# Graph layers on one core: the row of f by way of DRAM, the next batch taken up sooner, other buffer counts

## The chip, the core and the metric

The kernel runs on one core of a Trainium2 chip. Time is device microseconds (us) from start to end of one launch. The median of three runs of the kernel before is 2380.97 us (2374.90 to 2388.02). One further execution was taken with the hardware profiler; every row below comes from that one.

The core has five engines that run side by side, each through its own list of instructions in order: TensorE (PE, matrix products and transposes), VectorE (DVE), ScalarE (ACT), GpSimd (POOL) and SyncE (SP). SP only issues DMA transfers; POOL here issues the indexed ones (gathers and scatters), ACT the stores of the output. An instruction whose inputs are not there yet stops everything behind it on its own engine.

## The reference

Two graph layers on x of 16 batches x 1024 nodes x 256 features, with one 1024 x 1024 matrix `adj` that has few entries other than zero.

```
# layer 0, for each batch
feats  = data @ W1.T
f1     = feats @ W2 + b2[0]
logits = f1[:, None] + f1[None, :]
coefs  = softmax(leaky_relu(logits) + bias1, axis=-1)      # bias1 = adj
h      = coefs @ feats + bias2 + data
# layer 1, for each batch
hidden = relu((h @ W1[:d])[:, None, :] + (h @ W1[d:])[None, :, :] + b1)
S      = sigmoid(hidden @ W2 + b2)
a_t    = (S * adj).T @ h
m_t    = (adj.T @ h) * h
z      = beta1*h + beta2*(a_t @ Wa + ba) + beta3*(m_t @ Wm + bm)
```

Layer 0 is dense: each batch has a softmax over 1024 x 1024 logits. Each logit is a sum of one number per row and one number per column, so a tile of 128 rows of logits needs f of its own rows as a column (one number per partition, `f99`) and f of all 1024 nodes as a row that stands in every partition (`frow`). In layer 1, S is only needed where `adj` is not zero, so it is computed edge by edge.

## The kernel before

**Order.** The kernel writes its own schedule. A planner (`Timetable`) keeps a clock, `times.now`, that counts only PE's matmuls. Helpers such as `transposes`, `attention`, `one_end` put a PE step at `times.now` and move the clock on; what must follow on other engines is put at a due time after it (`times.at`). At the end all entries are emitted in order of due time. So the due times set the order of instructions on each engine, and nothing else; the hardware waits for whatever is late.

**Dense stage.** Batches 0 to 15 run one after the other. A batch `b` has these steps on PE:

- `begin(b, h)`: two times eight transposes of x into `xT` (L891). The tile of x, `xh` (`held[b]`), is loaded by `load_x` (L439) and later overwritten by h; there are two such tiles.
- `begin_features(b, c2)`, four times: products of `xT` with `w1T` (L926), whose last column gives f. `keep_features` cuts f to `f99` on DVE (L939), takes an exponential and scales on ACT (L943, L951).
- `begin_f(b)`: eight transposes of `f99`, broadcast, put f as a row into all 128 partitions in PSUM (`pr`, L911); ACT copies that to `frow` with a constant added (L919).
- for each of eight tiles of rows: `before` (ACT L962 adds f of the row and takes a relu, DVE L969 adds `adj`, ACT L975 takes the exponential), `transposes` (L981, copied to `eT` by ACT L985), `attention` (L991), and `keep_h` on DVE (L1002, L1005) which makes h.
- for each of four pairs of tiles: `turned_ends` (L1011, copied to `hT` by ACT L1022), `one_end` twice (L1028, stored to `pu_d` and `pw_d` through the doubled tiles `end0` and `end1`), `weigh_ends` (L1058, stored to `ha_d` through the doubled tile `ea`).
- `messages` (L1090) and `products` (L1110, DVE L1120 writes `zb`, which SP stores to `zb_d`). They read `held[b]` to the end.

The steps are interlaced: the last tiles of batch `b` run while batch `b+1` is turned and gets its features, and the messages and products of batch `b-1` run inside batch `b`. Batches 0 to 3 and 14 (`LATER`) are put off: h goes to DRAM (`put_off`, L1079), and their messages and products come much later, after `take_up` (L1083) has loaded h again. PSUM has two pools: `p1` with four tiles and `p2` with two; `begin`, `begin_features`, `begin_f` and `transposes` all use `p2`.

**Scores.** As soon as a group of four batches has its `pu_d` and `pw_d`, POOL gathers rows of them for 540 tiles of edges (L1144, L1151, eight buffers `gv`), DVE compares (L1180), DVE or ACT sums up (L1191, L1194), and POOL scatters the results to `sa_d` (L1160). This runs beside the dense stage from 386 us on, on all engines but PE.

**Gathering.** After the dense stage, for each group in the order 1, 2, 0, 3 and each of eight columns of tiles (`vc`), PE multiplies with S*adj in four parts (`gather`, L1284). Each part needs a piece of `sa_d` (`load_sa`, L1254, five buffers), turned so that the batches stand apart (`part_sa`, ACT L1267), weighed with `adj` on DVE (`weigh_sa`, L1272), and two tiles of `ha_g` (`load_ha`, L1249, `HA` = 11 buffers of 4 KB per partition, eight tiles to a group). The put-off messages and products stand between these parts (`follows`). Every column ends with `finish_z` (L1305) and a store.

At the end of a batch, PE's order before the change is: transposes 4, turned_ends 0, attention 3, transposes 5, attention 4, turned_ends 1, begin(b+1, 0), both_ends 0, begin(b+1, 1), transposes 6, attention 5, both_ends 1, features 0, transposes 7, attention 6, turned_ends 2, features 1, features 2, one_end(2, 0), features 3, half_end(2, 1, 0), attention 7, begin_f(b+1).

Of the kernel before, what the change touches and what calls it, by code (L numbers as in the profile page):

```python
# [14 lines left out]
P = 128  # L15
# [355 lines left out]
def edge_layers(  # L371
# [65 lines left out]
    def load_x(b):  # L437
        held[b] = dense.tile([P, C, D], F32, name="xh", bufs=2)
        nc.sync.dma_start(out=held[b], in_=x_view[b])  # L439
# [197 lines left out]
    ha_d = [dram.tile([N, G * D], F32, name=f"ha_d{g}") for g in range(NG)]  # L637
    h_d = {b: dram.tile([P, C * D], F32, name=f"h_d{b}") for b in LATER}
    zb_d = [dram.tile([N, G * D], F32, name=f"zb_d{g}") for g in range(NG)]

# [276 lines left out]
    def keep_f(b):  # L917
        st["frow"] = work.tile([P, N], F32, name="frow")
        nc.scalar.activation(st["frow"], st.pop("pr"), AF.Identity, bias=b2_s)  # L919

    def features(b, c2):
        pf = st["pf", c2] = p2.tile([P, 2, BANK], F32, tag="p2", name="pf")
        for i in range(2):
            c = 2 * c2 + i
            for h in range(H):
                nc.tensor.matmul(  # L926
                    pf[:, i, : D + 1],
                    lhsT=st["xT"][:, h, c * P : (c + 1) * P],
                    rhs=w1T[:, h, :],
                    start=(h == 0),  # L930
                    stop=(h == H - 1),
                )
# [148 lines left out]
    def take_up(b):  # L1081
        held[b] = dense.tile([P, C, D], F32, name="xh", bufs=2)
        nc.sync.dma_start(out=held[b].rearrange("p c d -> p (c d)"), in_=h_d[b])  # L1083
# [51 lines left out]
    AHEAD = 6  # L1135
    HA = 11
    SA = 5
# [123 lines left out]
    def part_sa(g, vc, part):  # L1261
# [4 lines left out]
        )  # L1266
        nc.scalar.copy(apart, sat.rearrange("p c v g -> p c g v"))  # L1267

# [57 lines left out]
    def begin_f(b):  # L1326

        end = times.matmuls(1024, lambda: rows_of_f(b))
        times.at(end + 0.1, lambda: keep_f(b))
        for c in range(3):  # L1330
            before(b, c, end + 1.5 + 2.5 * c)

    def begin_features(b, c2):
        end = times.matmuls(4 * (D + 1), lambda: features(b, c2))
        times.at(end + 0.3, lambda: keep_features(b, c2))

    def before(b, c, time):
# [59 lines left out]
    for b in range(B):  # L1397
# [28 lines left out]
        if b == 0:  # L1426
            for i in range(2):
                end_of = times.matmuls(512, lambda i=i: turn_columns(i))
                times.at(end_of + 0.3, lambda i=i: keep_columns(i))

        transposes(b, 2)
        before(b, 5, times.now)
# [15 lines left out]
        attention(b, 2)  # L1448
        time = products(b - 1, 2, 3) if at_once else times.now
        if more:  # L1450
            times.at(time, lambda b=b: load_x(b + 1))
        else:
            times.at(time, lambda: take_up(LATER[0]))

        transposes(b, 4)
        before(b, 7, times.now)
        turned_ends(b, 0)
        attention(b, 3)

        transposes(b, 5)  # L1460
        attention(b, 4)
        turned_ends(b, 1)
        if more:
            begin(b + 1, 0)
        both_ends(b, 0)

        if more:
            begin(b + 1, 1)
        transposes(b, 6)
        attention(b, 5)  # L1470
        both_ends(b, 1)
        if more:
            begin_features(b + 1, 0)

        transposes(b, 7)
        attention(b, 6)
        turned_ends(b, 2)
        if more:
            begin_features(b + 1, 1)
            begin_features(b + 1, 2)  # L1480
        else:
            times.now += 1.0
        one_end(b, 2, 0)
        if more:
            begin_features(b + 1, 3)
        half_end(b, 2, 1, 0)

# [115 lines left out]
    for n, (g, c) in enumerate((g, c) for g in order for c in range(C)):  # L1603
        if n < C:
            due = lead + 2.0 + PACE * (n + n // 2 + 1)
        elif n < HA:
            due = when[2 + n - C] + 0.1
        else:
            k, c1 = divmod(n - HA, C)
            due = when[C * 2 * k + (15 if c1 < C // 2 else 16)] + 0.1  # L1610
        times.at(due, lambda g=g, c=c: load_ha(g, c))
# [73 lines left out]
```

## Time and profile before

| what | value |
|---|---|
| three runs, median | 2380.97 us |
| profiled execution, whole | 2388.68 us |
| its span, first to last instruction | 2387.0 us |
| mean granted TensorE clock | 0.961 |
| moved by DMA | 638.19 MB, 267 GB/s over the span |
| `frow` written (L919), first of batch 1, batch 4, batch 5, batch 15 | 98.86, 306.92, 383.99, 1604.38 us |
| from one `frow` to the next, batches 1 to 4 | 69.1 to 69.6 us |
| from one `frow` to the next, batches 6 to 15 | 110 to 130 us, mean 122 us |
| gathering, first L1284 to the end | 1775.98 to 2387 us |

The busy time of PE is modelled from the start of each matmul, so a PE that is shown as busy need not be at its peak. The granted clock is the share of full speed at which the throttle let PE run in a stretch. In the rows, "a <- b" names what ended an engine's idle time.

### The profile page before, as it was taken

Reading aid. Unit: us, or ns where it says so; the run is one execution under the profiler, and the core shown is the slowest. Engines: PE = TensorE matmul, PEld = TensorE weight load, DVE = VectorE, ACT = ScalarE, POOL = GpSimd, SP = SyncE. Lnnn points to the kernel's source line nnn. Section 1 sums busy time; section 2 is a strip of 40 time slices with the busy share of each in tenths; the row PEclk is TensorE's granted clock in tenths of the full one; section 3 lists DMA queues with packets and bytes.
Section 4 is the critical chain, followed back from the end, with each engine's and each line's share of the span. In section 5 each row is a group of like instructions: output and inputs, shape, how many; then the busy total and the mean of one; then the engine's idle time right before and its main releaser. Section 6 shows DMA issues by size and latency. Waiting matters only on the chain.

```text
span 2387.0 us, 30406 instructions
## 1 busy us (share of the span) xinstructions
PE 2193.2 (92%) x9478; PEld 1684.9 (71%) x9478; DVE 1729.9 (72%) x2660; ACT 1467.0 (61%) x3820; POOL 1376.8 (58%) x1277
## 2 busy tenths in 40 slices
PE   7999999898987899999897998988889999999998
PEld 6888877676665576666675766667557768778687
DVE  6699658777776777777685777767558888879544
ACT  5544567475746565656474656657347778779554
POOL 2223125677775767666776666767656776777400
PEclk9999999999999999999998999989999999999999
DMA  6789887777776777777776777778799999999664
GB/s 235 272 313 335 307 319 234 233 231 237 241 235 208 234 223 241 227 229 233 225 247 228 236 217 221 230 220 272 255 322 392 354 354 404 340 395 405 228 213 150
DMA packets 282491, 638.19 MB, mean 267 GB/s; under 512 B 43218, under 2 KB 142546, under 8 KB 281042
## 3 DMA queue, kind: packets, MB, share of 16 engines
q0 software_dynamic: 109312, 349.81, 46.1%
q1 hardware_dynamic: 154450, 268.93, 31.2%
q10 hardware_dynamic: 18560, 17.44, 2.2%
q8 instruction: 77, 1.26, 0.2%
q14 instruction: 92, 0.75, 0.1%
HBM read 476.42 MB, written 159.78 MB: 267 GB/s over the span
## 4 chain that ended last, share of the span: by engine, by line
PE 59%; DVE 17%; another core or an unknown queue 6%; issue 6%; ACT 5%; DMA 4%; POOL 1%; SPq 0%; POOLq 0%; DVEq 0%; ACTq 0%
PE pzg L1284 16%; PE pm L1090 12%; PE pv L991 10%; PE pp L1028 7%; DVE gv L1180 6%; PE pf L926 3%; PE pz L1110 3%; PE pea L1058 3%; DVE lg L1191 2%; PE pt L981 2%; DMA xh<-in_x_dram 2%; DVE e L969 2%; ACT gv L1194 2%; ACT e L962 1%
## 5 line engine op out<-in xcount | busy, mean ns | idle before, releaser
L1151 POOL DMA_INDIRECT gv<-pw_d,idx_v x540 | 591.7, 1096 | 398.9 <-ACT gv L1194 200.0
L1194 ACT ACTIVATE gv<-gv 128x272 f32<-128x272 f32 x1380 | 576.5, 421 | 348.3 <-DVE gv L1180 216.1
L1180 DVE TENSOR_TENSOR gv<-gv,gu 128x544 f32<-128x544 f32 x1080 | 735.0, 719 | 0.0
L1160 POOL DMA_INDIRECT sa_d<-lg,idx_s x540 | 620.2, 1148 | 185.7 <-issue 154.3
L991 PE MATMUL pv<-feats,eT 128*128 128x257 f32 x2048 | 479.4, 385 | 26.7 <-issue 14.5
L1284 PE MATMUL pzg<-ha_g,apart 128*128 128x256 f32 x2048 | 452.0, 382 | 16.8 <-issue 9.6
L1090 PE MATMUL pm<-adj_sb,xh 128*128 128x512 f32 x1024 | 455.8, 599 | 7.9 <-issue 7.9
L991 PEld LDWEIGHTS pv<-feats,eT 128*128 128x128 f32 x2048 | 385.0, 192 | 93.6 <-issue 27.3
L1284 PEld LDWEIGHTS pzg<-ha_g,apart 128*128 128x128 f32 x2048 | 390.4, 191 | 81.6 <-issue 18.5
L1090 PEld LDWEIGHTS pm<-adj_sb,xh 128*128 128x128 f32 x1024 | 195.0, 192 | 236.9 <-issue 234.8
L1028 PE MATMUL pp<-wuv,hT 128*128 128x272 f32 x1024 | 274.6, 416 | 40.0 <-ACT hT L1022 18.3
L1267 ACT COPY apart<-sat 128x1024 f32<-128x1024 f32 x128 | 263.5, 2063 | 65.7 <-PE pzg L1284 51.4
L1028 PEld LDWEIGHTS pp<-wuv,hT 128*128 128x128 f32 x1024 | 200.7, 202 | 93.4 <-ACT hT L1022 23.8
L1194 ACT ACTIVATION_READ_ACCUMULATOR gv<-gv 128x1 f32 x1380 | 262.3, 190 | 0.0
L1191 DVE TENSOR_REDUCE lg<-gv 128x4 f32<-128x1088 f32 x195 | 250.5, 1284 | 5.3
L1272 DVE TENSOR_TENSOR apart<-apart,adj_sb 128x1024 f32<-128x1024 f32 x128 | 156.7, 1224 | 107.9 <-ACT apart L1267 91.9
L969 DVE CUSTOM_DVE_ANT_0 e<-e,adj_sb 128x1024 f32<-128x1024 f32 x128 | 156.2, 1222 | 89.3 <-ACT e L962 54.8
L962 ACT ACTIVATE e<-frow,f 128x1024 f32<-128x1024 f32 x128 | 146.6, 1146 | 94.1 <-remote 53.0
L829 POOL DMA_INDIRECT table_d<-rec,at x52 | 56.3, 1083 | 198.4 <-DVE rec L824 177.1
L985 ACT COPY eT<-pt 128x1024 f32<-128x1024 f32 x128 | 127.8, 999 | 52.6 <-remote 13.3
L975 ACT ACTIVATE e<-e,top 128x1024 f32<-128x1024 f32 x128 | 145.8, 1145 | 19.9 <-DVE top L969 19.3
L981 PE MATMUL pt<-ident,e 128*128 128x128 f32 x1024 | 137.2, 277 | 15.2 <-ACT e L975 8.1
(171 smaller groups left out, 1923.8 us busy)
## 6 DMA issues: line engine op xcount, KB each, us to landing
sa_d<-zero SPq DMA_DIRECT2D x128, 512.0 KB
sat<-sa_d SPq DMA_DIRECT2D x128, 512.0 KB
pu_d<-end SPq DMA_DIRECT2D x64, 272.0 KB
pw_d<-end SPq DMA_DIRECT2D x64, 272.0 KB
xh<-in_x_dram SPq DMA_DIRECT2D x16, 1024.0 KB
ha_d<-ea SPq DMA_DIRECT2D x64, 256.0 KB
zb_d<-zb SPq DMA_DIRECT2D x64, 256.0 KB
ha_g<-ha_d SPq DMA_DIRECT2D x32, 512.0 KB
```

Of the source, the lines that this page charges most:

```text
L969: nc.vector.tensor_tensor_reduce(e, e, adj_sb[:, c, :], -1.0, BIG, ALU.add, ALU.min, accum_out=top)
L981: nc.tensor.transpose(pt[:, j * P : (j + 1) * P], e[:, j * P : (j + 1) * P], ident)
L991: nc.tensor.matmul(pv[:, : D + 1], lhsT=eT[:, j, :], rhs=st["feats", b][:, j, :], start=(j == 0), stop=(j == C - 1),)
L1028: nc.tensor.matmul(pp[:, :R], lhsT=st["hTi", b, i][:, h, k * P : (k + 1) * P], rhs=wuv[:, side, h, :], start=(h == 0), stop=(h == H - 1),)
L1090: nc.tensor.matmul(pm, lhsT=held[b][:, c, h * P : (h + 1) * P], rhs=adj_sb[:, c, span], start=(c == 0), stop=(c == C - 1),)
L1151: nc.gpsimd.indirect_dma_start(out=gv, out_offset=None, in_=pw_d[g], in_offset=bass.IndirectOffsetOnAxis(ap=idx_v[:, t, s : s + 1], axis=0),)
L1160: dma = nc.gpsimd.indirect_dma_start(out=sa_d[g], out_offset=bass.IndirectOffsetOnAxis(ap=idx_s[:, t, s : s + 1], axis=0), in_=lg[:, i, :] ...
L1180: nc.vector.tensor_tensor(mv, mv, mu, op)
L1191: nc.vector.tensor_reduce(lg[:, i, :], one, AX.X, ALU.add)
L1194: nc.scalar.activation(one[:, j, :], one[:, j, :], AF.Copy, accum_out=lg[:, i, j : j + 1])
L1267: nc.scalar.copy(apart, sat.rearrange("p c v g -> p c g v"))
L1284: nc.tensor.matmul(st["pzg", g, vc][:, j, :], lhsT=apart[:, c, j, :], rhs=st["ha", g, 2 * part + c][:, j * D : (j + 1) * D], start=(part = ...
```

## The change

It has six parts.

1. For all batches but the first, `begin_f` no longer transposes f on PE and no longer copies it on ACT. Instead `spread_f`, right after the last features, adds the constant on DVE into a small tile `f_out`, and SP stores that to a row `f_d[b]` in DRAM; `take_f` loads that row into all 128 partitions of `frow`, also on SP. The `before` steps of the first three tiles are now due from the end of attention 7.
2. `xh` has three buffers instead of two, and `load_x(b+1)` is emitted ahead of transposes 2 instead of behind the last products of batch `b-1`.
3. The two `begin` steps move up: begin(b+1, 0) behind attention 3, begin(b+1, 1) behind turned_ends 1. The four `begin_features` are spread: behind transposes 6, behind attention 5, between the two ends of pair 1, and behind transposes 7.
4. The tail of the batch's order changes with that: pair 1's ends and weighing come between attention 5 and transposes 7, and turned_ends 2 comes before attention 6.
5. `ha_g` has nine buffers instead of eleven (two tiles of 4 KB make room for the third `xh` of 8 KB), and from the tenth load on its due time is 3.5 us after the start of the part that reads the buffer last.
6. `part_sa` reads `sat` in the order in which it lies and writes `apart` in steps of 128 elements; before, it read in steps of four elements and wrote in order.

```diff
-        held[b] = dense.tile([P, C, D], F32, name="xh", bufs=2)
+        held[b] = dense.tile([P, C, D], F32, name="xh", bufs=3)
...
+    f_d = [dram.tile([N, 1], F32, name=f"f_d{b}") for b in range(B)]
...
+    def spread_f(b):
+
+        f = two.tile([P, C], F32, name="f_out")
+        nc.vector.tensor_scalar(f, st["f99"], b2_s, None, ALU.add)
+        nc.sync.dma_start(out=f_d[b].rearrange("(c p) o -> p (c o)", p=P), in_=f)
+
+    def take_f(b):
+
+        st["frow"] = work.tile([P, N], F32, name="frow")
+        nc.sync.dma_start(
+            out=st["frow"], in_=f_d[b].rearrange("n o -> (n o)").partition_broadcast(P)
+        )
...
-    HA = 11
+    HA = 9
...
-        nc.scalar.copy(apart, sat.rearrange("p c v g -> p c g v"))
+        nc.scalar.copy(apart.rearrange("p c g v -> p c v g"), sat)
...
     def begin_f(b):
 
-        end = times.matmuls(1024, lambda: rows_of_f(b))
-        times.at(end + 0.1, lambda: keep_f(b))
+        if b == 0:
+            end = times.matmuls(1024, lambda: rows_of_f(b))
+            times.at(end + 0.1, lambda: keep_f(b))
         for c in range(3):
-            before(b, c, end + 1.5 + 2.5 * c)
+            before(b, c, times.now + 1.5 + 2.5 * c)
...
         times.at(end + 0.3, lambda: keep_features(b, c2))
+        if b and c2 == C // 2 - 1:
+            times.at(end + 0.6, lambda: spread_f(b))
+            times.at(end + 3.0, lambda: take_f(b))
...
+        if more:
+            times.at(times.now, lambda b=b: load_x(b + 1))
         transposes(b, 2)
...
-        time = products(b - 1, 2, 3) if at_once else times.now
-        if more:
-            times.at(time, lambda b=b: load_x(b + 1))
-        else:
-            times.at(time, lambda: take_up(LATER[0]))
+        if at_once:
+            products(b - 1, 2, 3)
+        if not more:
+            times.at(times.now, lambda: take_up(LATER[0]))
...
         attention(b, 3)
+        if more:
+            begin(b + 1, 0)
 
         transposes(b, 5)
         attention(b, 4)
         turned_ends(b, 1)
         if more:
-            begin(b + 1, 0)
+            begin(b + 1, 1)
         both_ends(b, 0)
 
-        if more:
-            begin(b + 1, 1)
         transposes(b, 6)
-        attention(b, 5)
-        both_ends(b, 1)
         if more:
             begin_features(b + 1, 0)
-
-        transposes(b, 7)
-        attention(b, 6)
-        turned_ends(b, 2)
+        attention(b, 5)
         if more:
             begin_features(b + 1, 1)
+        one_end(b, 1, 0)
+        if more:
             begin_features(b + 1, 2)
-        else:
-            times.now += 1.0
-        one_end(b, 2, 0)
+        one_end(b, 1, 1)
+        weigh_ends(b, 1)
+
+        transposes(b, 7)
         if more:
             begin_features(b + 1, 3)
+        turned_ends(b, 2)
+        attention(b, 6)
+        one_end(b, 2, 0)
         half_end(b, 2, 1, 0)
...
-            due = when[C * 2 * k + (15 if c1 < C // 2 else 16)] + 0.1
+            due = begins[order[k], C - 1, c1 // 2] + 3.5
```

More of the change, by code (lines that the diff above doesn't have):

```diff
@@ L1081, in take_up @@
     def take_up(b):
-        held[b] = dense.tile([P, C, D], F32, name="xh", bufs=2)
+        held[b] = dense.tile([P, C, D], F32, name="xh", bufs=3)
         nc.sync.dma_start(out=held[b].rearrange("p c d -> p (c d)"), in_=h_d[b])
```

## The prediction

> **What bounds the kernel now.** I read the busy shares first, then the stages, then TensorE's (PE's) idle times one by one, then the chain that ended last, and at the end the rows of what the diff touches. The page's first part, and the busy time of five stretches that I cut at the kernel's stages (batches 1 to 4; ten batches with messages; batch 15 and what is left of the dense work; gathering while scores still run; the last group alone):
>
> ```profile
> PE 2193.2 (92%) x9478; PEld 1684.9 (71%) x9478; DVE 1729.9 (72%) x2660; ACT 1467.0 (61%) x3820; POOL 1376.8 (58%) x1277
> ...
> 98.86:306.92 208.06, 205.65 (x1081) 177.53 (x1080) 166.21 (x275) 113.58 (x163) 48.46 (x44) 1.00 0.87 322
> 505.46:1604.38 1098.92, 982.49 (x4105) 722.98 (x4104) 807.29 (x1286) 663.09 (x2021) 755.76 (x680) 0.94 0.75 230
> 1604.38:1767.30 162.92, 143.18 (x540) 96.29 (x538) 102.72 (x168) 87.57 (x280) 107.61 (x104) 0.95 0.83 278
> 1767.30:2276.50 509.20, 492.36 (x2034) 382.20 (x2034) 403.94 (x485) 375.40 (x902) 336.07 (x282) 0.99 0.94 353
> 2276.50:2387.00 110.50, 103.59 (x480) 90.86 (x479) 53.99 (x47) 55.48 (x27) 0.00 (x0) 0.98 0.57 182
> ```
>
> PE is the bound in the early batches (205.65 of 208.06 us) and while gathering (492.36 of 509.20). In the ten long batches it works 982.49 of 1098.92 us at a granted clock of 0.94: there about a tenth goes to stalls. The chain says whose:
>
> ```profile
> PE 59%; DVE 17%; another core or an unknown queue 6%; issue 6%; ACT 5%; DMA 4%; POOL 1%; SPq 0%; POOLq 0%; DVEq 0%; ACTq 0%
> ...
> 804.60 12.57 another core or an unknown queue
> 824.65 11.45 DMA xh<-in_x_dram
> ...
> 1261.34 13.17 another core or an unknown queue
> 1296.10 11.21 DMA xh<-in_x_dram
> ```
>
> Most of the stall is the unlabelled kind (6% of 2387 us is about 150 us), in which DVE and ACT stand still for up to 13 us while POOL issues gathers; the diff touches none of its parts. The loads of x are the part that it does touch. PE's own waits there, and beside them the rows that the diff removes or alters:
>
> ```profile
> 344.39 1.94 PE L891 MATMUL pt<-ident,xh 128*128 128x128 f32 x8 [4.33 <-DMA xh<-in_x_dram]
> 836.24 1.94 PE L891 MATMUL pt<-ident,xh 128*128 128x128 f32 x8 [4.88 <-DMA xh<-in_x_dram]
> 1308.11 1.69 PE L891 MATMUL pt<-ident,xh 128*128 128x128 f32 x8 [4.04 <-DMA xh<-in_x_dram]
> ...
> L911 PE MATMUL pr<-ident,f 128*128 128x128 f32 x128 | 16.8, 273 | 1.6 <-issue 1.6
> L919 ACT ACTIVATE frow<-pr,b_s 128x1024 f32<-128x1024 f32 x16 | 17.8, 1111 | 24.0 <-PE pr L911 20.6 <-PE pv L991 1.7 <-issue 1.7
> L926 PE MATMUL pf<-w1T,xT 128*128 128x257 f32 x512 | 124.6, 389 | 11.2 <-issue 7.1 <-ACT eT L985 3.4 <-DVE xT L900 0.5
> L1267 ACT COPY apart<-sat 128x1024 f32<-128x1024 f32 x128 | 263.5, 2063 | 65.7 <-PE pzg L1284 51.4 <-DVE zg L1305 7.9 <-DMA sat<-sa_d 4.5
> L975 ACT ACTIVATE e<-e,top 128x1024 f32<-128x1024 f32 x128 | 145.8, 1145 | 19.9 <-DVE top L969 19.3
> ```
>
> **Part by part**, against the profiled execution (span 2387.0, whole 2388.68 us; the three runs have a median of 2380.97, 7.7 below it).
>
> **The f row off PE.** 15 of 16 batches lose the eight transposes of L911: 16.8 x 15/16 = 15.8 us of PE. Four boundaries lie where PE is full, 4 x 1.05 = 4.2 us, counted whole; the other 11.6 us lie among stalls, where I count only PE's share of the chain, 59%: 6.8. Together -11.0 (bounds 0 and -15.8). ACT loses 17.8 x 15/16 = 16.7 us of L919; ACT is busy 61%, so I count nothing for it.
>
> **The f row by DRAM: does it come in time?** Added per boundary: one DVE add (as f99's L939, 0.16 us, on an engine 72% busy: nothing), a store of 1024 single elements, and a load of 512 KB into 128 partitions. The load waits for the store on SP, so SP's queue stands; behind it are stores of `end`, `ea` and clears. Their tiles are doubled and next written one round later, so this is hidden; without that cover it is the length of the wait. The waiter that matters is ACT: `logits` is queued at 1.5 us after attention 7, ahead of the `ea` and `hT` copies and the scores' sums, and in order. Working time: features 3 now ends before turned_ends 2, attention 6, one_end, half_end and attention 7: 0.6+3.48+2.0+1.08+3.64 = 10.8 us before attention 7's end. At the early boundary at 167.23 us the first `e` was started 2.2 us after that end, its transposes on PE stand at 175.39 (7.1 us after, without L911), and the chain of `e` took 173.93-169.45 = 4.5 us, so ACT may start 2.6 us after: the budget is 13.4 us. Where messages follow (boundary at 873.79), PE wants `e` at 885.98, 11.1 after: budget 17.5.
> The chain: 1.0 (eviction of f99 and the add) + 0.4 (SP issue, rows of 0.36 to 0.38) + store + 0.4 + load. The store isn't in the trace. Near row below: a scatter of 128 packets landed on the chain in 3.23 us. Near row above: the ACT queue's small packets in the first microseconds, 1122 in 8 us beside a full queue, so 1024 in 7.3 us:
>
> ```profile
> 1222.36 3.23 DMA sa_d<-lg,idx_s
> 1159.40 4.38 DMA gu<-pu_d,key_u
> 1607.92 7.46 DMA gv<-pw_d,idx_v
> ...
> q1 hardware_dynamic: 1396, 1.68, 67.1%
> q10 hardware_dynamic: 1122, 0.16, 12.0%
> ```
>
> The load has the packets of the gathers, 4.38 to 7.46 us; in the early batches, under the clears, 1 MB of x took up to 21.48, so half of it 10.7. Sum: 9.4 to 16.6, early 9.4 to 19.8. The middle, 13.0, is within 17.5: nothing at the ten long boundaries. At the five short ones (into batches 1 to 4 and 15) 14.6 against 13.4 is 1.2 late: +6 (bounds 0 and 5 x 6.4 = +32).
> [...]
>
> **x a third buffer and loaded earlier.** At 824.65 and 1296.10 the load left right after a `zb` (L1120) that read the old buffer, and PE then waited 4.88 and 4.04 us; with 4.33 at 344.39 that is 13.3. The turns after these waits ran 1.94, 1.94 and 1.69 us instead of 1.04: 2.5 more. With three buffers and the load some 30 us of planned PE time sooner, the turn, now one attention and a turned_ends earlier, finds x: -15.7 (bounds 0, if the stall only moves, and the chain's 21.48+11.45+11.21 = -44).
>
> **Features spread.** PE waited 11.2 us before L926, mostly where two pairs followed each other on the doubled PSUM buffer. I take a quarter: -3 (0 to -10).
>
> **Nine `ha`.** The loads go out a half later or sooner, 32 in all as before. At a change of group the first new tile leaves 3.5 us into the last column's first gather and is needed after 6.9+3.45+6.9+7.9 = 25.1 us of PE work (gathers, products, opening): 21 us of lead. A `sat` load on the chain in the fullest stage took 15.13. Nothing (up to +5).
>
> **The apart copy**, reading straight and writing spread. The strided read costs 2063 ns where contiguous L975 costs 1145. No row shows a strided write by ACT: below, 128 x (1145-2063) = -117 us of ACT; above, the doubling again, 128 x 2063 = +264 of ACT. I take about the middle of 1145 and 2063. PE's waits for `apart` are only 7.2 us in that stage, so ACT's gain is worth -2 (0 to -7).
> [...]
>
> Sum: -11.0 + 6 - 15.7 - 3 + 0 - 2 = **-25.7**, so 2388.7 - 25.7 = 2363.0; less 7.7, **2355** against the median. The last group also needs the scores' end, 38 us before its start at 2276.5, of which load, copy and weighing take some 11: 27 us of room, and about 9 more if scores start sooner by what the early batches gain (4.2 + 4.3 + 0.9). So the sum fits, and much more would not. Own range 2332 to 2376: without the x chain's end the good bounds are -15.8-15.7-10-7 = -48.5, if the scores keep step; at the other end f late by half its bound, +16, and a third of the remaining -31.7 lost, -21: -5.
>
> **Rivals.**
> *Swallowed.* In the long batches the freed time goes into the unlabelled stalls and the scores' pace. For: 12% idle there, POOL with its issue gaps almost full; against: L891's waits are PE's own. Left: 4.2 + 4.3 + 0.9 in the early batches, less 6 for f: -3, about 2378.
> *f late.* ACT, the only reader of `frow`, stands at `logits` with the scores' sums behind it. It decides once store plus load exceed 11.6 us early (13.4-1.8) or 15.7 in the long batches. At 7 us over at all 15: +105 on -32; half covered by slack of ACT's other work, +52: 2381+20 = 2401, slower. For: 1024 tiny packets and full queues; against: the gathers' 4 to 7 us.
> *Spread writes dear.* ACT, busy 375 of 509 us while gathering beside scores, takes up to 96 more doublings, 96 x 2063 = +198: it becomes the bound, 375+198-509 = +64; in the last group 55+66-110 = +11; with -24 from the rest 2381+51 = 2432. It decides from a copy of 2063 + 134/96 = 3.5 us. [...]
> *More than the sum*: fewer of the 150 us of unlabelled stalls: 2325.
>
> **Numbers.** Forecast 0.52, swallowed 0.19, f late 0.17, dear writes 0.06, more 0.06. Faster or slower by 0.5% is 12 us, about what a measurement of this kernel can tell from no change. Faster (under 2369): 0.46 of the forecast, 0.06 more, 0.04 of swallowed = 0.56; same: 0.05+0.12+0.02 = 0.19; slower: 0.01+0.03+0.15+0.06 = 0.25. The range, 2320 to 2412, leaves out the dear writes and the tails.
>
> **What would show it.** L911 eight times only; no PE wait for `in_x_dram` after batch 0; `logits` idle before it charged to the load of `frow` under 2 us in the long batches; the apart copy's mean under 2063; pf's waits shorter; long batches of about 120 us instead of 122. Wrong if ACT waits for `frow` by more than 5 us at most boundaries, if the copy takes over 3 us, or if the unlabelled stalls grow.

## The result, and the profile after

| | median, us | lowest to highest | runs |
|---|---|---|---|
| before | 2380.53 | 2374.90 to 2388.02 | 4 |
| after | 2491.25 | 2475.83 to 2498.72 | 4 |

The ratio is 1.0438, with a 95% interval of 1.0399 to 1.0477: the change costs some 105 us, where 26 of gain were forecast. The profiled execution of the kernel after took 2498.4 us, with a span of 2496.7.

Lines below the diff's first insertions have moved: before's L891 is L892 after, and L911, L919, L926, L962, L975, L981, L991, L1022, L1028 and L1267 are L912, L920, L940, L976, L989, L995, L1005, L1036, L1042 and L1281. First, of the page after, the busy shares, and then the groups that answer to those shown of before (line, engine, operation, shapes, count; busy us and mean ns; idle time before them and what ended it):

```profile
PE 2216.8 (89%) x9358; PEld 1695.4 (68%) x9358; DVE 1729.4 (69%) x2675; ACT 1435.5 (57%) x3805; POOL 1386.5 (56%) x1277
...
L976 ACT ACTIVATE e<-frow,f 128x1024 f32<-128x1024 f32 x128 | 146.5, 1146 | 203.0 <-DMA frow<-f_d 155.4
...
q1 hardware_dynamic: 172210, 276.86, 32.3%
```

```profile
L912 PE MATMUL pr<-ident,f 128*128 128x128 f32 x8 | 1.0, 272 | 0.0
L920 ACT ACTIVATE frow<-pr,b_s 128x1024 f32<-128x1024 f32 x1 | 1.1, 1115 | 0.0
L940 PE MATMUL pf<-w1T,xT 128*128 128x257 f32 x512 | 124.4, 386 | 6.7 <-issue 3.1 <-ACT feats L965 2.4 <-ACT eT L999 0.6
L1281 ACT COPY apart<-sat 128x1024 f32<-128x1024 f32 x128 | 256.1, 2008 | 69.6 <-PE pzg L1298 50.1
```

The transposes of f and the copies of its row are gone but for batch 0, as the diff says. In their place ACT stands 155.4 us at the `logits`, for the load of `frow`. The page's third part counts 172210 - 154450 = 17,760 more packets on SP's queue than before. That is 1184 for each of the 15 boundaries (the places where one batch's tail meets the first logits of the next), 1024 of them the store's single elements.

Who waits behind that, from the table of waits after (engine, what, line, releaser: us in total, times, longest), and then SP's own queue:

```profile
ACT e L976 <- DMA frow<-f_d: 155.4, 15, 13.7
DVE e L983 <- ACT e L976: 151.3, 55, 11.4
PE pp L1042 <- ACT hT L1036: 62.6, 13, 8.4
PE pt L995 <- ACT e L989: 56.8, 13, 8.0
...
SPq L931 <- DMA f_d<-f_out: 136.5, 12, 15.2
```

All 15 boundaries wait, not five. PE pays in two places, and the timeline shows that they belong to different boundaries. At the five short ones (into batches 1 to 4 and 15) PE waits for `hT` at the products of `one_end` (L1042), 2 to 3 us after the first logits have started: 33.5 us in all. At the ten long ones it waits for `e` at its transposes (L995), 51.4 us in all. Together that is 84.9 us. The rest of the row for `hT`, 29 us, lies elsewhere: 27 of it in seven waits 15 to 18.5 us ahead of the first logits, before ACT comes to the late row (the kernel before had 16.2 us of that kind in three waits).

The stages again: from the first logits of batch 1 to those of batch 4, from those of batch 6 to those of batch 15, then gathering and the last group. The prediction calls the first two stretches of before "batches 1 to 4" and "ten batches"; by the starts of `frow` they hold three batches and nine.

```profile
104.20:334.48 230.28, 208.68 (x1056) 179.64 (x1056) 166.17 (x275) 109.73 (x160) 47.50 (x43) 0.95 0.92 293
556.59:1723.75 1167.16, 998.87 (x4016) 729.51 (x4016) 804.62 (x1293) 651.90 (x2013) 755.79 (x680) 0.91 0.75 221
1886.00:2386.00 500.00, 490.69 (x2033) 382.62 (x2034) 403.62 (x485) 363.65 (x902) 341.30 (x282) 0.99 0.96 359
2386.00:2497.00 111.00, 104.02 (x482) 91.22 (x481) 54.41 (x47) 53.91 (x27) 0.00 (x0) 0.99 0.56 181
```

All the loss is in the dense stage. From first logits to first logits a short batch takes 75.0 to 77.7 us instead of 69.0 to 69.6, a long one 129.6 on the mean instead of 122, and gathering starts near 1895 us instead of 1776. From there to the end the kernel takes 602 us instead of 611.

**One boundary closely.** The kernel before at the boundary shown in the prediction, PE and then ACT (start, length; in brackets the idle time before and its releaser):

```profile
170.27 1.08 PE L1028 MATMUL pp<-wuv,hT 128*128 128x272 f32 x4
171.62 3.93 PE L1028 MATMUL pp<-wuv,hT 128*128 128x272 f32 x16 [0.26 <-ACT hT L1022]
175.39 1.04 PE L981 MATMUL pt<-ident,e 128*128 128x128 f32 x8
```

```profile
169.45 1.15 ACT L962 ACTIVATE e<-frow,f 128x1024 f32<-128x1024 f32 x1
170.51 0.56 ACT L1069 COPY ea<-pea 128x512 f32<-128x512 f32 x1
170.97 0.59 ACT L1022 COPY hT<-ph 128x512 f32<-128x512 f32 x1
```

And the kernel after, at its boundary into batch 1: SP, ACT, PE.

```profile
87.58 0.37 SPq L926 DMA_DIRECT2D f_d<-f_out  x1
...
99.72 0.32 SPq L931 DMA_DIRECT2D frow<-f_d  x1
```

```profile
104.20 1.15 ACT L976 ACTIVATE e<-frow,f 128x1024 f32<-128x1024 f32 x1 [10.18 <-DMA frow<-f_d]
105.25 0.57 ACT L1083 COPY ea<-pea 128x512 f32<-128x512 f32 x1
105.72 0.59 ACT L1036 COPY hT<-ph 128x512 f32<-128x512 f32 x1
```

```profile
99.08 1.08 PE L1042 MATMUL pp<-wuv,hT 128*128 128x272 f32 x4
106.36 6.74 PE L1042 MATMUL pp<-wuv,hT 128*128 128x272 f32 x16 [6.20 <-ACT hT L1036]
112.93 1.04 PE L995 MATMUL pt<-ident,e 128*128 128x128 f32 x8
```

Read it from the store: it is issued at 87.58, and it has landed only when SP can issue the load at 99.72, 12.1 us later; the load is 4.5 us on its way. Logits start at 104.20. Already in the order of before, `hT` is copied 1.52 us after logits start, and PE wants it as the very next thing: before, it came 0.26 us late. After, the copy stands behind the late logits, and so PE can't even do the products that lie between attention 7 and the transposes of `e`. The transposes come 15.9 us after the end of attention 7 (at 97.07), where 7.1 was the pace before.

At a long boundary PE has messages (L1104) in between and comes to `e` first. This is the one into batch 10, ACT and then PE:

```profile
1065.38 1.15 ACT L976 ACTIVATE e<-frow,f 128x1024 f32<-128x1024 f32 x1 [11.03 <-DMA frow<-f_d]
```

```profile
1058.67 7.03 PE L1104 MATMUL pm<-adj_sb,xh 128*128 128x512 f32 x16
1071.55 1.97 PE L995 MATMUL pt<-ident,e 128*128 128x128 f32 x8 [5.85 <-ACT e L989]
```

Over all 15 boundaries the store keeps SP for 9.6 to 15.6 us, mean 11.95, and from the load's issue to logits are 4.3 to 9.3, mean 7.04.

### The profile page after: what moved, and what is told of

Read it like the earlier page. It is cut to its first block, busy times and chain, and to the rows that moved or that the text cites. A ratio compares the mean times of both kernels' runs of the same rounds, so it can differ in the third digit from the quotient of the medians.

```text
span 2496.7 us, 30232 instructions
## 1 busy us (share of the span) xinstructions
PE 2216.8 (89%) x9358; PEld 1695.4 (68%) x9358; DVE 1729.4 (69%) x2675; ACT 1435.5 (57%) x3805; POOL 1386.5 (56%) x1277
## 3 DMA queue, kind: packets, MB, share of 16 engines
q1 hardware_dynamic: 172210, 276.86, 32.3%
## 5 line engine op out<-in xcount | busy, mean ns | idle before, releaser
L1165 POOL DMA_INDIRECT gv<-pw_d,idx_v x540 | 601.8, 1115 | 455.8 <-ACT gv L1208 206.0
L1005 PE MATMUL pv<-feats,eT 128*128 128x257 f32 x2048 | 495.3, 391 | 32.9 <-issue 21.1
L1005 PEld LDWEIGHTS pv<-feats,eT 128*128 128x128 f32 x2048 | 391.5, 195 | 111.2 <-issue 48.0
L1104 PE MATMUL pm<-adj_sb,xh 128*128 128x512 f32 x1024 | 450.3, 593 | 3.4 <-issue 1.9
L1042 PE MATMUL pp<-wuv,hT 128*128 128x272 f32 x1024 | 288.8, 434 | 76.1 <-ACT hT L1036 62.6
L1104 PEld LDWEIGHTS pm<-adj_sb,xh 128*128 128x128 f32 x1024 | 193.5, 191 | 226.1 <-issue 224.0
L1042 PEld LDWEIGHTS pp<-wuv,hT 128*128 128x128 f32 x1024 | 211.7, 213 | 133.8 <-ACT hT L1036 71.5
L1281 ACT COPY apart<-sat 128x1024 f32<-128x1024 f32 x128 | 256.1, 2008 | 69.6 <-PE pzg L1298 50.1
L976 ACT ACTIVATE e<-frow,f 128x1024 f32<-128x1024 f32 x128 | 146.5, 1146 | 203.0 <-DMA frow<-f_d 155.4
L995 PE MATMUL pt<-ident,e 128*128 128x128 f32 x1024 | 148.9, 291 | 73.2 <-ACT e L989 56.8
L995 PEld LDWEIGHTS pt<-ident,e 128*128 128x128 f32 x1024 | 130.4, 152 | 100.4 <-ACT e L989 66.0
L1072 PE MATMUL pea<-wa,hT 128*128 128x256 f32 x512 | 136.9, 415 | 32.0 <-DVE end L1055 16.8
```

The lines of the kernel that those rows point to most:

```text
L995: nc.tensor.transpose(pt[:, j * P : (j + 1) * P], e[:, j * P : (j + 1) * P], ident)
L1005: nc.tensor.matmul(pv[:, : D + 1], lhsT=eT[:, j, :], rhs=st["feats", b][:, j, :], start=(j == 0), stop=(j == C - 1),)
L1042: nc.tensor.matmul(pp[:, :R], lhsT=st["hTi", b, i][:, h, k * P : (k + 1) * P], rhs=wuv[:, side, h, :], start=(h == 0), stop=(h == H - 1),)
L1104: nc.tensor.matmul(pm, lhsT=held[b][:, c, h * P : (h + 1) * P], rhs=adj_sb[:, c, span], start=(c == 0), stop=(c == C - 1),)
L1165: nc.gpsimd.indirect_dma_start(out=gv, out_offset=None, in_=pw_d[g], in_offset=bass.IndirectOffsetOnAxis(ap=idx_v[:, t, s : s + 1], axis=0),)
L1281: nc.scalar.copy(apart.rearrange("p c g v -> p c v g"), sat)
```

## The experiments

They ran on four chips, and each kernel is compared with the kernel before on its own chip: 2391.6 us on chip A, 2420.5 on B, 2210.1 on C, 2213.9 on D. Ratios are to that, with the 95% interval; where a single run was made, none is given.

| label | chip | us | ratio |
|---|---|---|---|
| e1_no_f | A | 2411.27 | 1.0069 [1.0037, 1.0100] |
| e2_f_only | A | 2580.35 | 1.0769 [1.0690, 1.0847] |
| e3_rows | A | 2396.29 | 1.0010 [0.9968, 1.0051] |
| e4_pieces | A | 2409.59 | one run |
| e5_late_turn | B | 2416.12 | 0.9979 [0.9947, 1.0010] |
| e7_x_only | B | 2418.03 | 0.9986 [0.9959, 1.0013] |
| e8_behind | B | 2481.73 | 1.0223 [1.0169, 1.0277] |
| e9_pairs | B | 2411.97 | one run |
| a0_after | C | 2294.60 | 1.0371 [1.0343, 1.0399] |
| e8b_behind | C | 2274.15 | 1.0287 [1.0260, 1.0315] |
| e10_old_order | C | 2197.24 | 0.9941 [0.9919, 0.9963] |
| e11_old_order_rows | C | 2233.28 | 1.0111 [1.0086, 1.0137] |
| e12_no_f | D | 2209.61 | 0.9975 [0.9953, 0.9997] |
| e13_late_turn | D | 2213.28 | 0.9987 [0.9965, 1.0009] |
| e14_old_order | D | 2198.91 | 0.9928 [0.9905, 0.9951] |
| e15_old_apart | D | 2198.99 | 0.9938 [0.9913, 0.9963] |

### Is it the f row? The change without it, and it alone

e1_no_f is the change with f transposed on PE for every batch:

```diff
-        if b == 0:
-            end = times.matmuls(1024, lambda: rows_of_f(b))
-            times.at(end + 0.1, lambda: keep_f(b))
+        end = times.matmuls(1024, lambda: rows_of_f(b))
+        times.at(end + 0.1, lambda: keep_f(b))
...
-        if b and c2 == C // 2 - 1:
-            times.at(end + 0.6, lambda: spread_f(b))
-            times.at(end + 3.0, lambda: take_f(b))
```

> The changed kernel with f turned on PE again for every batch (rows_of_f and keep_f; no spread_f, no take_f); everything else of the change stays. Theory A, the store of 1024 single elements is slow (11.9 us from its issue to the issue of the load, mean of 15) and ACT stands at the first logits of every batch (155.4 us in 15 waits): without it the time falls to 2350 to 2385 us, and PE's waits for hT and e at the start of a batch (119 us in the changed kernel) go. Theory B, the other parts of the change (order of the tail, three xh, nine ha) cost the time and the wait for f lies beside them: the time stays above 2460 us.

e2_f_only is the reverse: the kernel before, with `f_d`, `spread_f`, `take_f` and the new `begin_f` of the change, and nothing else of it.

> The kernel before with the f row by way of DRAM alone (spread_f, take_f, the logits due from the end of attention 7); order, buffers and the apart copy as before. Features 3 ends here only one half_end and one attention (some 4.6 us) before attention 7's end, 6 us less than in the changed kernel. Theory A: ACT waits some 6 us longer at each of 15 boundaries, 15 to 17 us each, and the time is 2500 to 2590 us. Theory B: the f row alone costs little, 2370 to 2400 us.

e1 lies between the two expectations: the f route costs 3.7% (1.0438 - 1.0069, some 88 us; the kernel after itself was not run on chip A), most of the loss, but the rest of the change does not gain on this chip; it costs 0.7%. e2 is worse than the whole change: in the tail of before only half_end and attention 7 stand behind features 3, so the row has less lead. ACT's wait for `frow` grew to 218.2 us (15 times, longest 17.9). The reordering is thus needed by the f route, and was not enough for it.

### Is it the store, and its pieces?

e3_rows turns `f99` on PE to eight rows (one transpose of 128 columns), adds the constant there, and stores eight rows of 512 bytes (the three lines in `begin_features` that called `spread_f` and `take_f` go):

```diff
-        f = two.tile([P, C], F32, name="f_out")
-        nc.vector.tensor_scalar(f, st["f99"], b2_s, None, ALU.add)
-        nc.sync.dma_start(out=f_d[b].rearrange("(c p) o -> p (c o)", p=P), in_=f)
+        f = two.tile([C, P], F32, name="f_out")
+        nc.vector.tensor_scalar(f, st.pop("pf8")[0:C, :P], b2_s[0:C, :], None, ALU.add)
+        nc.sync.dma_start(out=f_d[b].rearrange("(c p) o -> c (p o)", p=P), in_=f)
+
+    def turn_f(b):
+
+        pf8 = st["pf8"] = p1.tile([P, BANK], F32, tag="p1", name="pf8")
+        nc.tensor.transpose(pf8[0:C, :P], st["f99"], ident)
...
         turned_ends(b, 2)
+        if more:
+            end_f = times.matmuls(P, lambda b=b: turn_f(b + 1))
+            times.at(end_f + 0.2, lambda b=b: spread_f(b + 1))
+            times.at(end_f + 1.5, lambda b=b: take_f(b + 1))
```

> The changed kernel, but f99 (128x8) is first turned on PE to 8x128, with one transpose of 128 columns, and stored as eight rows of 512 B in place of 1024 single elements; the load stays. Theory A: from the store's issue to the load's issue 2.5 to 5 us instead of 11.9, the wait of ACT for frow under 3 us at a boundary, and a time of 2345 to 2385 us. Theory C, any way by DRAM is too slow, as two transfers stand in series in full queues: the store still takes over 8 us and the time stays above 2450 us.

e4_pieces stores the same bytes as 128 pieces of 32, and e9_pairs as 512 pieces of 8; in both the row holds f in another order:

```diff
-        nc.sync.dma_start(out=f_d[b].rearrange("(c p) o -> p (c o)", p=P), in_=f)
+        nc.sync.dma_start(out=f_d[b].rearrange("(p c) o -> p (c o)", p=P), in_=f)
```

> The changed kernel with f stored as 128 pieces of 32 B, one for each partition; the row that is loaded then has f in another order of the nodes (this changes the logits; no instruction more or less). Theory A: the number of elements sets the store's time: 2.5 to 5 us from the store's issue to the load's, and 2350 to 2390 us. Theory C: still over 8 us, and 2450 us or more. If 128 small pieces are as slow as 1024 elements, it is the small write itself and not their number.

```diff
-        nc.sync.dma_start(out=f_d[b].rearrange("(c p) o -> p (c o)", p=P), in_=f)
+        nc.sync.dma_start(
+            out=f_d[b].rearrange("(c p t) o -> p c (t o)", p=P, t=2),
+            in_=f.rearrange("p (c t) -> p c t", t=2),
+        )
```

> The changed kernel with f stored as 512 pieces of 8 B in place of 1024 of 4 B (the row that is loaded has f in another order of the nodes, which changes the logits and no instruction). 128 pieces of 32 B took 3.3 us from the store's issue to the load's (mean of 15), 1024 of 4 B 11.9. [...]

Means over the 15 boundaries of each profile:

| pieces | kernel | store's issue to load's issue, us | load's issue to logits, us |
|---|---|---|---|
| 8 of 512 B | e3_rows | 2.78 | 6.69 |
| 128 of 32 B | e4_pieces | 3.55 | 7.41 |
| 512 of 8 B | e9_pairs | 6.11 | 6.16 |
| 1024 of 4 B | after | 11.95 | 7.04 |

The bytes are the same 4 KB in each; the time follows the pieces, (11.95 - 6.11)/512 = 11 ns for each of the last 512. (The expectation of e9 has 3.3 us for 128 pieces; the mean of the 15 is 3.55. At one price for each piece from 128 to 1024, 512 would take an estimated 3.55 + 384/896 x 8.40 = 7.15 us; they took 6.11.) The last column is the load's own time only where ACT waits for it, which it does at all 15 boundaries of the kernel after but at seven of e3. There the wait for `frow` is 21.5 us instead of 155.4, and the time falls to that of before. e4 and e9 were single runs, 0.8% above and 0.4% below the kernel before of their chips. So the store's many small pieces are shown as the cause of the late row.

How the store spends its time is seen in the DMA's work after, while a store of f was under way (issued at 1046.99, the load behind it at 1056.55). First from 1047.85 to 1048.7 us, then from 1048.7 to 1056.5; the counts are of packets, then for each queue packets, MB and the share of the engines' time:

```profile
DMA packets 1051, 0.01 MB, mean 16 GB/s; under 512 B 1049, under 2 KB 1049, under 8 KB 1051
q1 hardware_dynamic: 1040, 0.00, 55.5%
```

```profile
DMA packets 42, 0.18 MB, mean 23 GB/s; under 512 B 0, under 2 KB 0, under 8 KB 42
q0 software_dynamic: 42, 0.18, 62.6%
```

All 1040 packets of SP's queue pass in 0.85 us. For the 7.8 us that follow the store has not landed, and hardly anything else moves either: 42 packets of POOL's queue, 23 GB/s, where the long batches have 221 on the mean. This boundary is no exception. In the last 6 us ahead of the load's issue, the core's DMA moves 22 to 70 GB/s at each of the 15, mean 38; in e3 it moves 106 to 346, mean 241. So the pieces are quick to leave, their landing takes the time, and meanwhile the store holds up the core's other transfers too. Why the landing takes so long, the trace does not show. What the held-up transfers cost apart from the late row was not tested either: no run has the pieces without the late row.

### What is f off TensorE worth when its row is in time?

e5_late_turn is e3 with `turn_f` behind attention 6, since in e3 PE waited 53.6 us before that one transpose (39.3 of it charged to `f99` on DVE, the rest to "issue").

> The kernel with eight rows of 512 B, with the turn of f one attention (3.5 us of PE) later, behind attention 6. In the run with the eight rows PE stood 53.6 us before that turn, for f99 that DVE had not yet cut. Theory D, this wait is PE's own loss: it goes, ACT's wait for frow rises from 21.5 us in all to at most 40, and the time is 10 to 30 us below the run with the eight rows (ratio to before 0.987 to 0.997). Theory E, DVE stands in the unlabelled stalls anyway, and the wait only moves to the next reader (hT, the ends, e): same time as the run with the eight rows, ratio 0.997 to 1.006.

e5 ran on chip B, where neither e3 nor e1 did, so it settles nothing here. Chip A: e3 against e1 is 15 us less, the 15.8 us of transposes, with intervals that overlap a little. On chip D the two sides were set against each other again, e12_no_f being e1 and e13_late_turn being e5:

> The change with f on TensorE in all batches (as e1_no_f), once more, beside the old order on one chip. If the tail order and the earlier turn cost time by themselves (N), it is 0.7% to 1.5% slower than e14_old_order here: the difference between 1.0069 and 0.9941, which came from two chips, is real. If the difference is one of chips (C), it is within 0.4% of e14_old_order here, and both are between 0.993 and 1.008 of the kernel before.

> The change with f stored as eight rows, turned behind attention 6 (as e5_late_turn). The f row off TensorE is worth its 15.8 us of transposes only if the load is hidden: then it lies 0.6% below e12_no_f on any chip (as 0.9979 against 1.0069 said). By C it is then also below e14_old_order; by N it is at or above e14_old_order (0.998 against 0.994).

There e13 is not below e12 (0.9987 against 0.9975, intervals overlapping), though PE's busy time fell from 2128.4 to 2118.3 us. The span without PE's busy time was 93.8 us instead of 79.5: PE stood idle for more than it had been spared. The boundary into batch 1, on ACT with the line of the table of waits, and then on PE:

```profile
98.23 1.15 ACT L981 ACTIVATE e<-frow,f 128x1024 f32<-128x1024 f32 x1 [3.71 <-DMA frow<-f_d]
...
ACT e L981 <- DMA frow<-f_d: 69.7, 15, 7.2
```

```profile
93.94 3.64 PE L1010 MATMUL pv<-feats,eT 128*128 128x257 f32 x16
97.42 1.89 PE L1077 MATMUL pea<-wa,hT 128*128 128x256 f32 x8
99.14 0.60 PE L1030 MATMUL ph<-ident,xh 128*128 128x128 f32 x4
99.58 4.82 PE L1047 MATMUL pp<-wuv,hT 128*128 128x272 f32 x20
104.24 1.04 PE L1000 MATMUL pt<-ident,e 128*128 128x128 f32 x8
```

At this boundary ACT waits 3.71 us and PE not at all: logits start 0.65 us after attention 7's end (93.94 + 3.64 = 97.58), and `hT` is there when PE comes to it. Here the wait of ACT was no loss. So what f off PE gains lies between nothing and 15 us, by chip, even with a store a quarter as long.

### What stands behind the waiting logits?

e8_behind is the kernel after, with the first three logits of every batch but the first due 3.8 us instead of 1.5 after attention 7, so that the copies of `ea` and `hT` and the evictions of `end` go first on ACT. It ran on chip B, and as e8b_behind on chip C beside a0_after, the kernel after unaltered.

```diff
-            before(b, c, times.now + 1.5 + 2.5 * c)
+            time = times.now + 3.8 + 2.5 * c
+            times.at(time, lambda c=c: logits(b, c))
+            times.at(time + 1.1, lambda c=c: add_adj(b, c))
+            times.at(time + 2.7, lambda c=c: exponentials(b, c))
```

> The changed kernel, with the logits of the first three tiles due 3.8 us after attention 7 in place of 1.5, so that they stand behind the copies of ea, hT and the last end on ACT. Theory H, half or more of the cost of the late row comes from what is queued behind the waiting logits: PE's 62.6 us of waits for hT go, and the time falls by 30 us or more, to below 2460. Theory I, e itself is late, so PE comes to stand at the transposes of e in place of hT: 2475 to 2500 us, and PE's waits for e grow by about what those for hT lose.

> The changed kernel once more, so that the three beside it have it on their own chip: ratio to before 1.040 to 1.048, as first measured.

> The changed kernel with the logits behind the copies of ea, hT and the last end, again. On another chip it stood at a ratio of 1.0223 to before, where the changed kernel had 1.0438. Theory H, what is queued behind the waiting logits is half of the cost: ratio 1.017 to 1.028 here too, with the changed kernel at 1.044 beside it. Theory I, the difference came from the chip: within 0.5% of the changed kernel.

On chip C the 20 us between the two are about a quarter of the loss (0.84 of 3.71%). The waits of a0_after and then of e8b_behind:

```profile
ACT e L976 <- DMA frow<-f_d: 142.4, 15, 15.5
PE pt L995 <- ACT e L989: 43.8, 9, 8.7
PE pp L1042 <- ACT hT L1036: 28.8, 8, 7.2
```

```profile
ACT e L976 <- DMA frow<-f_d: 57.4, 12, 8.6
PE pt L995 <- ACT e L989: 51.1, 17, 5.8
```

PE's wait for `hT` has fallen to 3.2 us, that for `e` has grown and now stands at the short boundaries too: the products no longer stand still, but `e` is late. So the order on ACT made the late row dearer, and the lateness itself is the greater part. This order on ACT does not mend it.

### The rest of the change: order, x, and the apart copy

e7_x_only is the kernel before with three `xh`, `load_x` ahead of transposes 2, and nine `ha` with their due times; the old tail, f on PE, the old apart copy. e10_old_order adds the new apart copy to it. e11_old_order_rows is e10 with e3's eight rows, turned behind half_end(2, 1, 0).

```diff
-        held[b] = dense.tile([P, C, D], F32, name="xh", bufs=2)
+        held[b] = dense.tile([P, C, D], F32, name="xh", bufs=3)
...
-    HA = 11
+    HA = 9
...
+        if more:
+            times.at(times.now, lambda b=b: load_x(b + 1))
         transposes(b, 2)
```

> The kernel before with three xh, the load of x ahead of transposes 2 and nine ha; order of the tail, f on PE and the apart copy as before. Theory F, PE's waits for x are worth what they show: those at the long batches (4.88 and 4.04 us, with the slow turns behind them) go, 5 to 15 us less than before, ratio 0.993 to 0.998. Theory G, a long batch's length is set by the scores beside it and the unlabelled stalls: ratio 0.998 to 1.003. If the ratio is over 1.004, the buffers themselves cost, and the order of the tail is not what made the changed kernel without f by DRAM 0.7% slower than before.

> The kernel before with three xh, the early load, nine ha and the apart copy, but the tail's order and f on PE as before. Theory J, the order of the tail costs what the changed kernel without f by DRAM lost (ratio 1.0069), and the apart copy gives the 8 us by which all gathering stages with it are shorter (602 to 606 us from the first gather to the end, against 611 to 614): ratio 0.992 to 0.997. Theory K, the tail's order is neutral and three xh or nine ha cost: 1.002 to 1.008.

> The same, with the f row by DRAM as eight rows of 512 B, turned behind the half_end that follows features 3. Only 4.5 us of PE work lie between features 3 and attention 7's end, and the chain (0.9 + 1.0 + 0.4 + 2.8 + 0.4 + 4.5 = 10 us) ends some 4 us after the logits' place in ACT's queue. Theory L, waits of ACT under some 4 us cost nothing (512 pieces left 53 us of them, 3.5 at a boundary, at no cost), and PE's 15.8 us of transposes are the gain: 0.6% under the run without it, ratio 0.985 to 0.992. Theory M, the wait costs in full here: ratio 0.996 to 1.003.

On chip B the x part is not told from nothing; on chip C, with the copy, 0.6% are gained. e11 with its ACT wait of 103.0 us in 15 (longest 9.8) gives back 1.7%: the old tail leaves the row too little lead. As e10 and e1 had run on different chips, e12, e14_old_order (e10) and e15_old_apart (e7) were run side by side on chip D.

> The kernel before with three xh, load_x ahead of transposes 2, nine ha and the apart copy of the change; old tail order, f on TensorE (as e10_old_order, 0.9941 on the fastest chip). By N faster than before by 0.3% to 0.8% on this chip too, and the best of the four. By C about as e12_no_f.

> e14_old_order with the apart copy of the kernel before (as e7_x_only, 0.9986). If the apart copy's 8 us in the gathering stage reach the whole time, it is 0.3% to 0.5% above e14_old_order; if scores or the order of the last group swallow them, the two are equal within 0.15%.

Three things follow. The tail order costs by itself: e12 and e14 differ only in it (and in where the x tiles are turned), by 10.7 us, with intervals that do not meet. The x part with nine `ha` gains 0.6% here (e15, 13.7 us by the ratio). And the apart copy changes nothing in the whole time (2198.99 and 2198.91). A part of the order's cost is seen at the turn of batch 5's x, in e12 and then in e14:

```profile
348.56 1.94 PE L892 MATMUL pt<-ident,xh 128*128 128x128 f32 x8 [9.33 <-DMA xh<-in_x_dram]
```

```profile
344.31 1.94 PE L891 MATMUL pt<-ident,xh 128*128 128x128 f32 x8 [4.39 <-DMA xh<-in_x_dram]
```

The load takes 22 us there in both and starts at 326.02 and 321.89. Turned sooner, x isn't there. That is 5 of the 16 us by which e12 is behind at the first logits of batch 15 (1465.3 against 1449.2 us in the two profiles); the remainder lies in steps of up to 7 us, not all of one sign, at single batches and was not traced to single waits, and some of it is made up by the end.

The kernel of e10 and e14 is the fastest of the study (e15 equals it without the apart copy), faster than before by 0.6% and 0.7% on the two chips where it ran. On chip C it beats the kernel after as well, which did not run on D; on B, its x part alone (e7) was not told from no change.

## Why the prediction was wrong

**What bounds the kernel** held: PE in the early batches and while gathering, stalls in between.

**The step that failed is the store's bound, "Near row above".** It took 1122 packets in 8 us on ACT's queue as the slow end for 1024 single elements, 7.3 us. These were packets of another kind (0.16 MB in 1122, some 140 B on the mean) and of several transfers; nothing made them an upper end. The store took 9.6 to 15.6 us, mean 11.95, and all 15 exceeded the bound. The load was near the rows given for it: 4.3 to 4.5 us to logits at the first four boundaries, 6.9 to 9.3 later, where 7.46 was the slower row. From the store's issue to logits that is 19.0 us on the mean, where the whole chain had 13.0 as its middle and 16.6 as its end. Hence "nothing at the ten long boundaries" fell as well: there these two alone take 19.8, past even the budget of 17.5. The prediction also had no term for what the store does to other transfers, which it holds up for most of its time (the 38 GB/s above); what that costs stays open.

**The budget was 1.6 us too large at the short boundaries,** and that was in plain sight in the trace of before. It was reckoned to PE's transposes of `e`, as if PE's products in between ran meanwhile. But they read `hT`, whose copy is queued behind logits on ACT and came 0.26 us late as it was. PE wants it at 170.4 without L911, and 2.16 us pass from the start of logits to `hT` (104.20 to 106.36), so logits must start at 168.2, 1.0 after attention 7 and not 2.6: a budget of 11.8 us. The prediction named the `ea` and `hT` copies as queued behind logits and didn't ask who waits for them. e8b shows that part as about a quarter of the loss. Check it at the boundary into batch 1: logits started at 104.20, 7.1 us after attention 7 where 1.0 was needed, so 6.1 late, and PE's wait there is 6.20. At the long boundaries PE comes to `e` first, as the prediction had it. There the reader was right, but the store and the load were too small (11.7 and 8.1 us on the mean, where the middles were 5.3 and 5.9): 51.4 us of waits, some 5 a boundary, where nothing was put down. All 15 give the 84.9 us of above, against 88 to 104 lost (the f route's 88 net, and up to 16 more for the transposes that it removed); the difference was not traced. The term had been +6, with +32 as its end.

**The rival "f late"** had the mechanism, the place and nearly the threshold (11.6 us early). It was sized by "7 us over at all 15, half covered by slack of ACT's other work": the lateness was about right, the cover wasn't there. ACT's slack did not help: into batch 1 PE had nothing left in its queue ahead of the products that read `hT`, and stood 6.20 us.

**f off PE, -11 (0 to -15.8).** Inside the bounds: -15 on chip A, nothing on D.

**x, -15.7.** The waits of the long batches are gone after, as forecast. But the boundary into batch 5, which the sum also took as cured, got worse, since the turn moved up and the load there did not. PE came to the turn 29.2 us after the batch's first logits instead of 32.0, and the load left after 15.8 us instead of 14.7:

```profile
375.15 1.94 PE L892 MATMUL pt<-ident,xh 128*128 128x128 f32 x8 [11.45 <-DMA xh<-in_x_dram]
```

In the whole time, the part is worth 13.7 us on chip D and 3.4 on chip B, where the interval includes zero. The size was right only where the unlabelled stalls are missing (below); "swallowed" describes chip B.

**Features spread, -3.** PE's waits at those products did fall, 11.2 to 6.7 us. The tail order that goes with it costs 10.7 us on D, so the two together have the wrong sign; the spreading alone was not run. The prediction priced only the wait that the spreading relieves, and not what the other steps of the tail lose by being moved.

**Nine `ha`: nothing.** e15 and e7 have them and are not slower than before; they were not run without the third `xh`.

**The apart copy, -2.** I took the middle of 1145 and 2063 ns for the strided write; it took 2008 in the kernel after, and 2005 against 2065 in e14 against e15. Read or written in steps, the copy is as dear to within 3%. With its 8 us of ACT the whole time doesn't move on chip D. The gathering stage is 9 us shorter after than before (602 against 611), but on D it takes 604.5 us with the new copy and 599.3 with the old in the profiles of e14 and e15, so that gain isn't shown to be the copy's.

## What to carry to other kernels

Here the store of 4 KB took 11.95 us in 1024 pieces and 2.78 in eight, and 7.3 us, taken from 1122 packets of some 140 B on the mean, was no upper end for the 1024. So price a trip through DRAM by its pieces, take a row of another transfer as an upper bound only if its pieces are as small and as many, and turn the data on chip first, so that the store has a few long rows. When a wait is put on an engine, take the budget from the first reader of *anything* queued behind it, not from the reader of the late thing (here 11.8 us and not 13.4, as `hT` stood behind the logits). And a step that is moved earlier needs its load moved as far, at the shortest batch and not the typical one (PE waited 11.45 us for x at batch 5 after, 4.33 before).

## What the hardware showed that was not expected

The same kernel before took 2380.5, 2391.6, 2420.5, 2210.1 and 2213.9 us by chip. On one of the faster two, chip D, the profile of e14_old_order has none of the unlabelled stalls. For nine long batches (6 to 14), e7_x_only on chip B and e14_old_order on chip D, which differ by the apart copy of the later stage only (stretch, its length, busy time of PE, weight loads, DVE, ACT and POOL, granted clock, DMA share, GB/s):

```profile
513.00:1639.00 1126.00, 989.98 (x4099) 725.35 (x4098) 805.35 (x1285) 664.28 (x2028) 757.45 (x679) 0.94 0.73 224
```

```profile
486.00:1449.00 963.00, 934.50 (x4115) 702.74 (x4114) 806.19 (x1283) 662.33 (x2024) 757.35 (x675) 0.99 0.83 261
```

DVE, ACT and POOL are busy for the same time to within 2 us, and the stretch is 163 us shorter. "Another core or an unknown queue" holds 7% of the chain of e7 and none of e14's. What makes these stalls was not found. With them on chip B the x part was worth 3.4 us, without them on D 13.7, so a change of half a per cent has to be judged beside the kernel before on one chip.

A store of 1024 elements of 4 bytes took some 12 us where the same 4 KB in eight rows took under 3. At the boundary looked at, its packets had passed within 1.7 us of the issue; it was the landing that took the rest, and in that time the core's other transfers nearly stood still, at 23 GB/s.
